# Feed-forward units of all tokens, and the features' quad at the end of the dense run, in an adaLN block with linear attention

## The chip, the cores and the metric

One core of a Trainium2 chip. The metric is the device time of one execution in microseconds; lower is better. All data are fp32, and TensorE runs each fp32 matmul as two passes (the trace shows two matmul instructions for each in the code). TensorE is PE in the profile, VectorE DVE, ScalarE ACT, GpSimd POOL, SyncE SP (it issues nearly all DMAs).

## What is computed

A transformer block on x of 2 x 2048 x 256: LayerNorm with a learned scale and shift, causal linear attention with 16 heads of 16 channels and 128 random features, a gated residual, a second LayerNorm, and a feed-forward layer with 4 low-rank experts of which each token takes 2. Cut to what matters:

```python
phi(z)  = exp(z @ omega - 0.5 * |z|^2) / sqrt(128)          # per head
S, Z    = cumsum(phi_k * v), cumsum(phi_k)                  # causal, over tokens
y       = (phi_q @ S) / (phi_q . Z + 1e-6)
x       = x + ga * (y @ W_proj + b_proj)
h       = layernorm(x) * (1 + cb) + sb
w       = softmax(h @ Wg.T + bg), kept for the top 2 of 4 experts
out_e   = relu(h @ Wi.T + (h @ A_e.T) @ B_e.T) @ Wo.T       # hidden size 1024
x       = x + gb * sum_e w_e * out_e
```

Since only two experts count for a token, the kernel computes `relu(base + low_0)` and `relu(base + low_1)`, scales the input so that the first has weight 1, multiplies the second by rho (the ratio of the two weights), and adds them before the second layer.

## The kernel before

The tokens are worked in 8 blocks of 512 (i = 0 to 7), the heads in 4 groups of 4, and each block in 8 rounds (k = 0 to 7): a round is one head group and two chunks of 128 tokens. `keep_written_order` ties every engine to the order of the code, so what is written first on an engine runs first.

A round has a part of *dense* matmuls (full 128 x 128 array; `run_full`) and a part of *tiled* ones: `scores` (L481, four column tiles; for the next round's chunks), and `outputs` (L503: the sums for the states, ps, L521; on VectorE the new states S, L529 and L531; then the products with the scores, L538, and with the states, L544). ScalarE copies the result (y, L550). Then come the *features* of a later group, a quad of four matmuls on four row tiles (L446), whose exponentials ScalarE takes (L457), and the masks of the scores on VectorE (L497).

The dense part works on three blocks at once. For a = i + 1 it makes queries and keys (`query_key`, L350: matmul, VectorE's scaling L361, ScalarE's Square L364, two DMAs to DRAM) and values (`values`, L420); for i it transposes the keys (`turn`, which is `keys` L464 and the copy `keep_keys` L475); for p = i - 1 `project`, `norm2_stats`, `channels2` (transposes, then L322 on VectorE), `router`, `choose` (some 20 small VectorE instructions that pick the experts), `low_rank` (transposes of choose's result, L693), `weigh` (L701); for q = i - 2 the second feed-forward layer `finish` (L765, one token tile: 16 passes, then L777 on VectorE).

The first feed-forward layer runs in four *units* per block: half of its 8 channel tiles for half of its 512 tokens. A unit is `hidden` (L726: four banks, 8 matmuls of 256 columns), `first` (`low_step` on four row tiles, L721; four Relus on ScalarE, L749) and `second` (`low_step` again, four products with rho on VectorE, L762, four adds on GpSimd, L763). Units 1 to 3 of block q run in rounds 0, 1, 2 and unit 0 of block p in round 7; in between stand values and `turn`.

PSUM has eight banks: two hold the scores, four have the tag "mm" (`mm_tile`), two the tag "side" (`side_tile`). A unit takes all four mm banks, and so do the features. `outputs` takes both side banks; query_key, values, project and finish take one each; `turn` takes two of either kind, as it is told.

`behind(i, 5)` issues `choose(p)` and then `norm1_stats(i + 2)` on VectorE. After the last block, units, `finish` and `finish_last` of the last two blocks follow in a tail.

```python
run_full(i, k, turn)
if k == 5 and i:
    router(i - 1, mm_tile if i in (1, N - 1) else side_tile)
...
if following:
    scores(*following)
outputs(i, g, (t, t + 1))
gi, gg = divmod(n // NT + 1 + k % 2, NG)
if gi < N:
    exponentials(*features(gi, gg, k % 2))
```

Of the kernel before, what the change touches and what calls it, by code (L numbers as in the profile page):

```python
# [32 lines left out]
def kernel(  # L33
# [469 lines left out]
    def outputs(i, g, ts):  # L503

        sums, ys = (side_tile(f"{nm}{i}_{g}{ts[0]}") for nm in ("ps", "py"))
        rows = [slice(j * HW, (j + 1) * HW) for j in range(HG)]
        cols = [slice(j * VW, (j + 1) * VW) for j in range(HG)]
        v = st[i]["v"]  # L510
        before, added = [], []
        for t in ts:
            s0 = (t % 2) * P
            ps, kt = sums[:, s0 : s0 + HG * VW], turned.pop((i, g, t), None)
            before.append(None if i % NBLK == 0 and t == 0 else S[g])
            if kt is None:
                continue
            for j in range(HG):
                for c in range(4):
                    cg = slice(c * CG, (c + 1) * CG)  # L520
                    nc.tensor.matmul(  # L521
                        ps[cg, cols[j]], kt[:, j, cg], v[:, t, g * HG + j, 0:VW],
                        start=True, stop=True,
                    )
            S[g] = work.tile([P, HG * VW], FP, tag=f"S{g}", name=f"S{i}_{g}{t}", bufs=3)
            added.append((S[g], ps, before[-1]))
        for new, ps, old in added:
            if old is None:
                nc.vector.tensor_copy(new, ps)  # L529
            else:  # L530
                nc.vector.tensor_add(new, ps, old)  # L531
        if ts[0] == 0:
            y[g] = work.tile([P, TB], FP, tag="y", name=f"y{i}_{g}")
        for t, state in zip(ts, before):
            tok = slice(t * P, (t + 1) * P)
            py, am = ys[:, (t % 2) * P : (t % 2 + 1) * P], staged.pop((i, g, t))
            for j in range(HG):
                nc.tensor.matmul(  # L538
                    py[rows[j], :], v[:, t, g * HG + j, :], am[:, j, :],
                    start=True, stop=state is None,  # L540
                )
            if state is not None:
                for j in range(HG):
                    nc.tensor.matmul(  # L544
                        py[j * HW : j * HW + VW, :], state[:, cols[j]], phi[i, g, 0, j][:, tok],
                        start=False, stop=True, tile_position=(0, j * HW),
                    )
        for t in ts:
            tok, py = slice(t * P, (t + 1) * P), ys[:, (t % 2) * P : (t % 2 + 1) * P]
            nc.scalar.copy(y[g][:, tok][:, ::-1] if t % 2 else y[g][:, tok], py)  # L550
        if ts[-1] == NT - 1:
            if g == 0:
                st[i]["ydr"] = dram.tile([NG, HG, 2, DH, TB], FP, tag="ydr", name=f"ydr{i}")
            nc.sync.dma_start(st[i]["ydr"][g].rearrange("j s d t -> (j s d) t"), y[g])
# [168 lines left out]
                start=False, stop=True, skip_group_check=True, tile_position=(HW * j, 0),  # L723
            )

    def hidden(i, u, banks=None):  # L726

        s = st[i]
        f0, t0 = RG * (u % 2), TH * (u // 2)
        ts = slice(t0, t0 + TH)  # L730
        banks = [b[:, 0:TH] for b in banks or [mm_tile(f"ph{i}_{u}{j}") for j in range(RG)]]
        for j, ph in enumerate(banks):
            f = f0 + j
            for k in range(KC):
                nc.tensor.matmul(  # L735
                    ph, wi_sb[:, k, f * P : (f + 1) * P], s["h2"][:, k, ts],
                    start=(k == 0), stop=False, skip_group_check=True,
                )
        s["unit"][u] = (banks, f0, ts)

    def first(i, u):
        s = st[i]
        banks, f0, ts = s["unit"][u]
        low_step(s, 0, banks, f0, ts)
        r = [
            work.tile([P, 2, TH], FP, tag="r", name=f"r{i}_{u}{n}") for n in range(2)
        ]
        for j, ph in enumerate(banks):
            nc.scalar.activation(r[j // 2][:, j % 2, :], ph, AF.Relu)  # L749
        s["unit"][u] = (banks, f0, ts, r)  # L750

    def second(i, u):

        s = st[i]
        banks, f0, ts, r = s["unit"].pop(u)
        low_step(s, 1, banks, f0, ts)
        for j, ph in enumerate(banks):
            f = f0 + j
            if f not in s["g"]:
                s["g"][f] = work.tile([P, TB], FP, tag="g", name=f"g{i}_{f}", bufs=NF)  # L760
            g = s["g"][f][:, ts]
            nc.vector.scalar_tensor_tensor(g, ph, 0.0, s["rho"][:, ts], ALU.max, ALU.mult)  # L762
            nc.gpsimd.tensor_add(g, g, r[j // 2][:, j % 2, :])  # L763

    def finish(i, t, tile=side_tile, f0=0, f1=NF):  # L765

# [72 lines left out]
    def run_full(i, k, turn):  # L839


        a, p, q = i + 1, i - 1, i - 2
        late = a == N
        unit = None
        if (q >= 0 and k < 3) or (p >= 0 and k == 7):
            unit = (q, k + 1) if k < 3 else (p, 0)
        n = ({1: 2, 2: 0, 3: 3, 7: 1} if i == 0 else {0: 2, 1: 0, 2: 3, 7: 1}).get(k)
        if i == 0 and k == 0:
            values(0, 2)
            values(0, 3)  # L850
        if a < N and k == (i == 0):
            channels1(a)

        turned_here = (i, k) in ((0, 1), (1, 0), (1, 4))
        if turned_here:
            turn(mm_tile if k < 2 else side_tile)
        if p >= 0 and k == 3:
            project(p, 0, NT)
            norm2_stats(p)
        if q >= 0:  # L860
            t = ({4: 2, 6: 3} if late else {4: 0, 5: 1, 6: 2, 7: 3}).get(k)
            if t is not None:
                finish(q, t)
                if t == 3:
                    store(q)
        if p >= 0:
            if k == 4:
                channels2(p)
            elif k == 6 and q >= 0:
                low_rank(p)  # L870
        t = ({4: 0, 5: 1, 6: 2, 7: 3} if i == 0 else {0: 0, 1: 1, 2: 2, 7: 3}).get(k)
        if p >= 0 and k == 7:
            if q < 0:
                query_key(a, n)
                low_rank(p)
                values(a, t)
            weigh(p)
            if q < 0:
                turn(side_tile)
                turned_here, n, t = True, None, None  # L880
        last_keys = (0, 1)
        if late and unit and k < 3:

            if k == 0:
                turn(side_tile, (0,))
                last_keys = (1,)
            else:
                finish(q, k - 1, side_tile, 0, RG)
        if unit and k == 0:
            hidden(*unit)  # L890
        if a < N and n is not None:
            query_key(a, n)
        if unit and k:
            hidden(*unit)
        if unit:
            first(*unit)
        if late and k in (1, 2):
            finish(q, k - 1, None, RG)
        if a < N and t is not None:
            values(a, t)  # L900
        if i == 0:
            if k in (4, 5):
                gate(k - 4, 0)
            elif k == 6:
                columns(1)
        elif i == 1 and k in (1, 4):
            gate(k // 4, 1)
        if not turned_here:
            on_side = unit or (k == 5 and (late or i == 1)) or (i, k) == (1, 6)
            turn(side_tile if on_side else mm_tile, last_keys)  # L910
        if unit:
            second(*unit)

    def amid(i, k):

# [41 lines left out]
    for i in range(N):  # L957
        for k in range(PAIRS):
# [7 lines left out]
                    keep_keys(i, g, t + n)  # L966

            run_full(i, k, turn)
            if k == 5 and i:
                router(i - 1, mm_tile if i in (1, N - 1) else side_tile)  # L970
            following = [chunk_at(m) for m in (n + 2, n + 3)] if n + 2 < TOTAL else []
            if following:
                scores(*following)
            outputs(i, g, (t, t + 1))

            gi, gg = divmod(n // NT + 1 + k % 2, NG)
            if gi < N:
                exponentials(*features(gi, gg, k % 2))
            for chunk in following:
                mask(*chunk)  # L980
# [13 lines left out]
        return pa + [side_tile(f"{name}{n}") for n in range(2)]  # L994

    divide_invert(p)
    hidden(q, 1, other_set("last1"))
    first(q, 1)
    hidden(q, 2)
    second(q, 1)  # L1000
    first(q, 2)
    hidden(q, 3, other_set("last3"))
    second(q, 2)
    first(q, 3)
    divide(p)
    finish(q, 0, mm_tile)
    second(q, 3)
    project(p, 0, NT)
    norm2_stats(p)
    finish(q, 1, mm_tile)  # L1010
# [7 lines left out]
    store(q)  # L1018
    low_rank(p)
    weigh(p)  # L1020
    hidden(p, 0)
    first(p, 0)
    hidden(p, 1, other_set("end1"))
    second(p, 0)
    first(p, 1)
    hidden(p, 2)
    second(p, 1)
    first(p, 2)
    hidden(p, 3, other_set("end3"))
    second(p, 2)  # L1030
    first(p, 3)
    finish_last(p, 0, 0, NF)
    second(p, 3)
    finish_last(p, 1, 0, NF)
    for f0 in (0, RG):
        for t in (2, 3):
# [48 lines left out]
```

## Time and profile before

| | us |
|---|---|
| median of 3 runs | 807.51 (801.08 to 807.72) |
| the profiled execution | 797.27 |
| its span, first to last instruction | 795.5 |
| TensorE busy, matmuls | 762.6 |
| VectorE, ScalarE, GpSimd busy | 381.8, 323.5, 137.6 |
| mean granted TensorE clock | 0.996 |

A block takes about 93 us in the middle of the kernel. The profile is of one execution. A group's "mean ns" is the duration of one instruction; matmuls are pipelined, so neighbours overlap and the distance from start to start is shorter (216 ns for a 256-column pass whose own duration is shown as about 380 ns). "[0.32 <-DVE v L431]" at the end of a line says that the engine sat idle for 0.32 us before it, and what ended that.

### The profile page before, as it was taken

To read this page: it belongs to the slowest core of one execution; us is meant where nothing else is said; L and a number is where in the kernel's file an instruction comes from. 1 tells how busy PE (TensorE), PEld (TensorE's weight loads), DVE (VectorE), ACT (ScalarE), POOL (GpSimd) and SP (SyncE) were. 2 spreads that over 40 slices of the span, in tenths; PEclk is the share of its full clock that TensorE was granted. 3 is DMA by queue.
4 is the path that set the end of the run, shared out by engine and by line. 5 is a ranking of instruction groups with operands and counts; after the bars stand their busy time and mean duration, and the time that the engine had idled before them with its cause. 6 is when DMAs were issued, how large, how long until landed. Compare 5 with 4: busy or idle time off the path is not lost.

```text
span 795.5 us, 30312 instructions
## 1 busy us (share of the span) xinstructions
PE 762.6 (96%) x13648; PEld 560.4 (70%) x13648; DVE 381.8 (48%) x1068; ACT 323.5 (41%) x700; POOL 137.6 (17%) x182
## 2 busy tenths in 40 slices
PE   9988999899999999999999999999999999999998
PEld 6555767476787667766687667777677767777766
DVE  5735558734445435543456344354364324543622
ACT  2644545434343354444444344444444343432020
POOL 3100300112101311121201121013130012004122
PEclk9999999999999999999999999999999999999999
DMA  4477243033221342023321332213230130012000
GB/s 127 123 232 247 77 153 115 23 92 108 69 82 47 104 132 84 16 82 113 105 69 36 95 105 81 69 49 115 85 106 16 55 98 16 16 42 70 2 26 28
DMA packets 44257, 65.84 MB, mean 83 GB/s; under 512 B 6752, under 2 KB 20256, under 8 KB 44128
## 3 DMA queue, kind: packets, MB, share of 16 engines
q1 hardware_dynamic: 42240, 62.33, 24.8%
q8 instruction: 107, 1.75, 0.9%
q10 hardware_dynamic: 1888, 1.58, 0.6%
q14 instruction: 22, 0.18, 0.1%
HBM read 35.32 MB, written 28.57 MB: 80 GB/s over the span
## 4 chain that ended last, share of the span: by engine, by line
PE 88%; DVE 4%; issue 3%; ACT 0%; ACTq 0%
PE pf L772 12%; PE ph L735 12%; PE pa L488 9%; PE pp L446 9%; PE pq L354 7%; PE pk L470 6%; PE ph L721 5%; PE ps L521 4%; PE py L538 4%; PE po L597 4%; PE py L544 4%; PE pv L427 4%; PE pf L794 2%; PE pw L707 1%; PE ptf L311 1%
## 5 line engine op out<-in xcount | busy, mean ns | idle before, releaser
L457 ACT ACTIVATE phi<-pp,lnm 128x512 f32<-128x512 f32 x256 | 154.9, 688 | 41.5 <-PE pp L446 41.5
L763 POOL TENSOR_TENSOR g<-g,r 128x256 f32<-128x256 f32 x128 | 90.4, 738 | 364.2 <-DVE g L762 324.5
L772 PE MATMUL pf<-wo_g,g 128*128 128x256 f32 x448 | 104.5, 385 | 0.2 <-DVE g L762 0.2
L735 PE MATMUL ph<-h,wi_sb 128*128 128x256 f32 x448 | 102.3, 381 | 1.8 <-DVE h L712 1.5
L772 PEld LDWEIGHTS pf<-wo_g,g 128*128 128x128 f32 x448 | 82.7, 190 | 29.0 <-issue 14.1
L735 PEld LDWEIGHTS ph<-h,wi_sb 128*128 128x128 f32 x448 | 84.0, 190 | 22.6 <-issue 5.1
L550 ACT COPY y<-py 128x128 f32<-128x128 f32 x128 | 27.8, 269 | 163.0 <-PE py L544 158.7
L488 PEld LDWEIGHTS pa<-phi,phi 128*32 128x32 f32 x4096 | 77.2, 110 | 14.9 <-issue 13.4
L478 ACT COPY kt<-pk 128x512 f32<-128x512 f32 x120 | 66.8, 592 | 49.6 <-PE pk L470 48.8
L488 PE MATMUL pa<-phi,phi 128*32 128x64 f32 (+3 forms) x4096 | 86.1, 235 | 0.0
L497 DVE TENSOR_TENSOR am<-pa,causal 128x512 f32<-128x512 f32 x128 | 82.3, 681 | 6.6 <-PE py L538 5.6
L446 PE MATMUL pp<-f,om 32*128 32x512 f32 x512 | 78.4, 655 | 0.6 <-issue 0.6
L470 PE MATMUL pk<-ident,phi 128*128 128x128 f32 x480 | 67.7, 276 | 1.5
L762 DVE SCALAR_TENSOR_TENSOR g<-ph,rho 128x256 f32<-128x256 f32 x112 | 39.6, 416 | 60.2 <-PE ph L721 60.2
L470 PEld LDWEIGHTS pk<-ident,phi 128*128 128x128 f32 x480 | 55.1, 141 | 16.3 <-issue 5.8
L544 PE MATMUL py<-phi,S 128*17 128x128 f32 x960 | 54.3, 275 | 10.0 <-issue 6.8
L749 ACT ACTIVATE r<-ph 128x256 f32<-128x256 f32 x112 | 34.0, 387 | 72.2 <-PE ph L721 62.9
L354 PE MATMUL pq<-hT,w_sb 128*128 128x512 f32 x120 | 59.6, 619 | 2.3 <-issue 1.8
L538 PE MATMUL py<-am,v 128*32 128x128 f32 x1024 | 56.4, 276 | 2.3 <-issue 2.2
L521 PE MATMUL ps<-v,kt 128*32 128x17 f32 x3840 | 48.7, 186 | 5.2 <-issue 4.3
L531 DVE TENSOR_TENSOR S<-ps,S 128x68 f32<-128x68 f32 x112 | 25.6, 228 | 54.2 <-PE ps L521 52.3
L431 DVE TENSOR_TENSOR v<-pv,bv_bc 128x256 f32<-128x256 f32 x32 | 13.5, 424 | 75.9 <-PE pv L427 75.6
(144 smaller groups left out, 834.2 us busy)
## 6 DMA issues: line engine op xcount, KB each, us to landing
f<-qd SPq DMA_DIRECT2D x60, 256.0 KB
qd<-qs SPq DMA_DIRECT2D x58, 256.0 KB
ydr<-y SPq DMA_DIRECT2D x32, 256.0 KB
num<-ydr SPq DMA_DIRECT2D x16, 256.0 KB
inv<-rdr SPq DMA_DIRECT2D x16, 256.0 KB
xt<-in_x_dram SPq DMA_DIRECT2D x7, 512.0 KB
out_dram<-xt SPq DMA_DIRECT2D x7, 512.0 KB
wo_g<-in_woT_dram SPq DMA_DIRECT2D x2, 1024.0 KB
```

The lines of the kernel that those rows point to most:

```text
L354: nc.tensor.matmul(pq, w_sb[:, k, n * P : (n + 1) * P], s["hT"][:, k, :], start=(k == 0), stop=(k == KC - 1),)
L446: nc.tensor.matmul(pp, om[rs, :], f[rs, :], start=True, stop=True, tile_position=(2 * DH * j, 0))
L457: nc.scalar.activation(ph, pps[j], AF.Exp, bias=lnm)
L470: nc.tensor.transpose(pk[:, j * P : (j + 1) * P], phi[i, g, 1, j][:, t * P : (t + 1) * P], ident)
L488: nc.tensor.matmul(pa[t % 2][c * CG : (c + 1) * CG, j * P + q0 : j * P + q1], phi[i, g, 1, j][:, t0 + c * CG : t0 + (c + 1) * CG], phi[i, ...
L497: nc.vector.tensor_mul(am, pa[t % 2][:].rearrange("p (h q) -> p h q", h=HG), causal[t % 2][:].unsqueeze(1).to_broadcast([P, HG, P]),)
L521: nc.tensor.matmul(ps[cg, cols[j]], kt[:, j, cg], v[:, t, g * HG + j, 0:VW], start=True, stop=True,)
L538: nc.tensor.matmul(py[rows[j], :], v[:, t, g * HG + j, :], am[:, j, :], start=True, stop=state is None,)
L544: nc.tensor.matmul(py[j * HW : j * HW + VW, :], state[:, cols[j]], phi[i, g, 0, j][:, tok], start=False, stop=True, tile_position=(0, j * HW),
L735: nc.tensor.matmul(ph, wi_sb[:, k, f * P : (f + 1) * P], s["h2"][:, k, ts], start=(k == 0), stop=False, skip_group_check=True,)
L763: nc.gpsimd.tensor_add(g, g, r[j // 2][:, j % 2, :])
L772: nc.tensor.matmul(po, s["g"][f][:, t * P : (t + 1) * P], wo_g[i // NBLK][:, f, :], start=(f == 0), stop=(f == NF - 1), skip_group_check=True,
```

## The change

Two things. First, the units: blocks whose units run inside the rounds have two *large* units (half of the channel tiles for all 512 tokens, so matmuls, Relus, products and adds of 512 columns), in round 1 of block q and in round 7 of block p; rounds 0 and 2 have none. In a large unit two of the four products are kept back and issued in `outputs`, behind the updates of S. The last block and the tail keep units of 256 tokens. Second, the features: where `ahead` holds, which is in all rounds without a unit, they are issued right after `run_full`, ahead of `router`, `scores` and `outputs`, and their exponentials stand ahead of the y copies on ScalarE. The dense part is now a table of steps, and with it the order in the dense part and the choice of banks for `turn` change: values of a block go to rounds 1 and 7 (two each), `finish` to rounds 2, 4, 6 and 7, and in rounds 2, 4, 5 and 6 the keys use side banks.

```diff
@@ outputs, behind the updates of S
+        for keep, j in kept_back:
+            keep(j)
+        kept_back.clear()
@@ units
-        f0, t0 = RG * (u % 2), TH * (u // 2)
-        ts = slice(t0, t0 + TH)
+    def small(u):
+        return RG * (u % 2), TH * (u // 2), TH
+    def large(u):
+        return RG * u, 0, TB
+        f0, t0, w = unit
+        ts = slice(t0, t0 + w)
@@ first
-            work.tile([P, 2, TH], FP, tag="r", name=f"r{i}_{u}{n}") for n in range(2)
+            work.tile([P, 2, w], FP, tag="r", name=f"r{i}_{f0}{t0}{n}") for n in range(2)
@@ second
-        for j, ph in enumerate(banks):
+        def keep(j):
...
+            nc.vector.scalar_tensor_tensor(g, banks[j], 0.0, s["rho"][:, ts], ALU.max, ALU.mult)
             nc.gpsimd.tensor_add(g, g, r[j // 2][:, j % 2, :])
+        now = RG if w < TB else RG // 2
+        for j in range(now):
+            keep(j)
+        kept_back.extend((keep, j) for j in range(now, RG))
@@ run_full
+        mm, side = (turn, mm_tile), (turn, side_tile)
         if i == 0:
+            steps = (
+                (mm, (values, 0, 2), (values, 0, 3)),
+                ((channels1, a), mm, (qk, 2)),
+                (mm, (qk, 0)),
+                (mm, (qk, 3)),
+                (mm, (gate, 0, 0), (v, 0)),
+                (mm, (gate, 1, 0), (v, 1)),
+                (mm, (columns, 1), (v, 2)),
+                (mm, (qk, 1), (v, 3)),
+            )
+        elif i == 1:
+            steps = (
+                ((channels1, a), mm, (qk, 2), (v, 0)),
+                (mm, (gate, 0, 1), (qk, 0), (v, 1)),
+                (mm, (qk, 3)),
+                (mm, (projection,)),
+                ((gate, 1, 1), side, (channels2, p)),
+                (side,),
+                (side,),
+                ((low_rank, p), (v, 2, 3), (weigh, p), side, (unit, p, large(0), (qk, 1))),
+            )
+        elif a < N:
+            steps = (
+                ((channels1, a), mm, (qk, 2)),
+                ((qk, 0), (unit, q, large(1), (v, 0, 1), side)),
+                ((qk, 3), side, (ff, 0)),
+                (mm, (projection,)),
+                ((ff, 1), (channels2, p), side),
+                (side,),
+                ((ff, 2), (low_rank, p), side),
+                ((ff, 3), (weigh, p), (qk, 1), (unit, p, large(0), (v, 2, 3), side)),
+            )
+        else:
+            steps = (
+                ((turn, side_tile, (0,)), (unit, q, (RG, 0, TH), (turn, side_tile, (1,)))),
+                ((ff, 0, side_tile, 0, RG),
+                 (unit, q, (RG, TH, TH), (ff, 0, None, RG), side)),
+                ((ff, 1), side),
+                (mm, (projection,)),
+                ((ff, 2), (channels2, p), side),
+                (side,),
+                ((ff, 3), (low_rank, p), side),
+                ((weigh, p), (unit, p, small(0), side)),
+            )
@@ the round
             run_full(i, k, turn)
+            gi, gg = divmod(n // NT + 1 + k % 2, NG)
+            ahead = not (k == 7 and i >= 1 or i >= 2 and k == 1 or i == N - 1 and k == 0)
+            if gi < N and ahead:
+                exponentials(*features(gi, gg, k % 2))
             if k == 5 and i:
-                router(i - 1, mm_tile if i in (1, N - 1) else side_tile)
+                router(i - 1)
...
             outputs(i, g, (t, t + 1))
-            gi, gg = divmod(n // NT + 1 + k % 2, NG)
-            if gi < N:
+            if gi < N and not ahead:
                 exponentials(*features(gi, gg, k % 2))
```

In a unit's step, what stands behind the unit's name runs between `first` and `second`; `ff` is `finish` of block q (and `store` after tile 3), `v` is `values` and `qk` `query_key` of block a.

## The prediction

> **What bounds the kernel now.** I read the page first (engine totals, the chain that ended last, the groups), then the waits of TensorE, then the timeline of single stretches of the fifth block (i = 4, 340 to 445 us), and last a place in the final block that already runs in the new order.
>
> ```profile
> PE 762.6 (96%) x13648; PEld 560.4 (70%) x13648; DVE 381.8 (48%) x1068; ACT 323.5 (41%) x700; POOL 137.6 (17%) x182
> ...
> PE 88%; DVE 4%; issue 3%; ACT 0%; ACTq 0%
> ```
>
> TensorE is busy 96% of the span and is 88% of the chain. In the waits of TensorE by releaser nearly all is "issue" (6.8, 4.3, 2.2 and 1.8 us), and all that names another engine is under 10 us. So the sum is simple: TensorE time taken out is gained, and every new wait of TensorE is lost in full. VectorE (48%) and ScalarE (41%) matter only where they return a PSUM bank or an operand too late. There are six banks to give: four "mm" and two "side". A tile gets a bank when its former user has been read out.
>
> **What it takes out**, per block of 8 rounds (i = 2 to 5). Start to start in the trace, a dense pass of 256 columns takes 216 ns and one of 512 takes 429 (each fp32 matmul is two passes). `hidden`: 64 x 216 becomes 32 x 429 ns, 13.82 to 13.73, 0.1 us. `low_step`: a quad of 256 columns takes 0.645 us (391.36 to 392.01); the features' quad, the same kind at 512 columns, 1.07. Eight quads become four: 5.16 to 4.28, 0.9 us. Moving the features: the last pass before a change between dense and tiled matmuls is 93 ns longer (309 for 216, 202 for 109). Dense to row tiles goes from 8 changes to 10, dense to column tiles from 4 to 0: 0.2 us. That outputs are now followed by dense work costs nothing: the last state quad takes 0.36 us before the features and also at the one place where dense work follows (698.89 to 699.26). In each round with a unit, the second key transpose waits about 0.3 us for VectorE to read the values (0.32 at 390.78) and the first starts 0.1 late; two such rounds instead of four save 0.8. Together 2.0 us per block.
>
> The Trainium skill ("TensorEngine Tiling (Array Packing)", Key Properties) says that a change of tiling mode drains TensorE, which gives the 93 ns a reason and speaks for the change; it names no price. Counted by that rule alone, the block falls from 36 changes to 30, and at the row's 93 ns the whole change would be worth 0.6 us a block.
>
> **What it adds: rounds 1 and 7 (the units).** Of the unit's four products, two are made before the S updates and two behind them; only then are the four mm banks free for the features, which stay last in these rounds. The same place in round 2 before (columns: start, duration, engine, line, operation):
>
> ```profile
> 392.01 1.33 PE L488 MATMUL pa<-phi,phi 128*32 128x128 f32 x64
> 392.10 1.42 DVE L762 SCALAR_TENSOR_TENSOR g<-ph,rho 128x256 f32<-128x256 f32 x4 [1.37 <-PE ph L721]
> ...
> 393.96 0.23 DVE L529 COPY S<-ps 128x68 f32<-128x68 f32 x1 [0.45 <-PE ps L521]
> 394.23 0.23 DVE L531 TENSOR_TENSOR S<-ps,S 128x68 f32<-128x68 f32 x1
> ...
> 394.59 1.14 PE L446 MATMUL pp<-f,om 32*128 32x512 f32 x8
> ```
>
> Count from the start of scores (392.01). The four products of 256 columns are done at +1.50, well before the features at +2.58. A product of 512 columns isn't in this trace. Its nearest row is L497, PSUM times SBUF over 128x512: 681 ns, 0.60 apart (two in 1.28); the other bound is two of L762, 0.67 apart. I take 0.60. Two run from +0.09 to +1.37 and delay nothing; S ends at +2.45 as before; the other two end at +3.05 and +3.65. The fourth matmul of the features' quad waits for the last bank until about +3.73 instead of starting at 2.58: 1.15 us (1.1 to 1.3), twice a block: 2.3. Behind that matmul stands the whole next round on TensorE; behind the two late products on VectorE stand the masks (and `divide`), which are read a round later. The Relus grow from 387 ns to about 592 (L478, a copy of 512 columns, is the nearest row; 0.57 apart): 2.4 us, under two values and two transposes of 3.0 us: nothing; without that cover it would be 0.6. GpSimd's adds (738 ns for 256 columns) may double to 1.5 us, so 5.9 us per unit; the second layer comes some 8 us later: nothing.
>
> Against this edit stands a rule: "If Scalar/Vector aren't saturated, but are causing bubbles on other engines, breaking up instructions may allow work to be completed sooner" (Trainium skill, "Perfetto Trace Analysis", Optimizing Scalar/DVE Operations). By that page's 125 ns per VectorE instruction on PSUM, merging would save 0.5 us of VectorE a unit (an estimate), and the wait would be nearer 0.9 than 1.15 us.
>
> **Round 2** is now query_key, transposes on side banks, finish of tile 0. Side banks alternate: the query takes one, the first transpose the other, the second transpose waits for the query's, `finish` for the first transpose's.
>
> ```profile
> 383.12 1.98 PE L354 MATMUL pq<-hT,w_sb 128*128 128x512 f32 x4
> ...
> 385.20 0.75 DVE L361 TENSOR_SCALAR qs<-pq,bqk 128x512 f32<-128x512 f32 x1 [2.28 <-ACT phi L457]
> ...
> 385.98 0.63 ACT L364 ACTIVATE qs<-qs 128x512 f32<-128x512 f32 x1 [0.36 <-DVE qs L361]
> ```
>
> From the query's start (0): its matmuls take 1.72 us, the first transpose 0.44, so the second could start at 2.16. VectorE has the query at 2.83, so it starts at 2.9: 0.75 lost. ScalarE's Square stands ahead of the key copy in its queue: Square to 3.49, copy (592 ns) to 4.0. `finish` could start at 3.34 and starts at 4.07: 0.73 lost. Together 1.5 us (0.75, if a bank of the other tile came first). Before, 3.55 us of `hidden` lay in between.
>
> **Round 6.** `low_rank` needs `choose`, 20 VectorE instructions at the end of round 5. Before, the features' quad (1.07) and `finish` (3.56) covered them, to the tenth of a microsecond:
>
> ```profile
> 421.96 3.72 PE L772 MATMUL pf<-wo_g,g 128*128 128x256 f32 x16
> ...
> 425.10 0.46 DVE L682 COPY los<-los 128x216 f32<-128x216 f32 x2
> ...
> 427.80 0.42 DVE L777 TENSOR_TENSOR xt<-pf,xt 128x256 f32<-128x256 f32 x1
> ```
>
> The features now come before the scores, so `finish` alone covers. The last block has no features in round 5, and shows what that costs:
>
> ```profile
> 699.26 3.72 PE L772 MATMUL pf<-wo_g,g 128*128 128x256 f32 x16
> ...
> 703.68 1.09 PE L693 MATMUL pl<-ident,los 128*128 128x128 f32 x8 [0.70 <-DVE los L682]
> ```
>
> 4.42 us from the start of `finish` to `low_rank`, not 3.56: 0.86 lost. Then the keys go to side banks, and the second transpose needs the bank of `finish`. Its reader (L777) stands behind choose and norm1_stats on VectorE and ended at 428.22, 7.33 us after the round-5 outputs ended (420.89); TensorE is there at 5.73. The loss is 1.67; it is 1.1 if that tile gets the first transpose's bank instead, whose copy waits behind two lT copies (L698); 0 if neither. I take 1.25, so 2.1 for the round. The mm banks that the keys used before were free.
>
> **Small ones.** Round 4: the features' fourth bank waits for the second h2 transpose (read out at 409.71, 5.72 us after its `finish` began; TensorE is there at 5.40): 0.4. Round 5: the second transpose waits for y copies that end 0.57 us after the outputs, 0.44 after its partner: 0.2. Rounds 0 and 3: nothing; exponentials end before the outputs, and divide's DMAs keep 5 us of slack (ydr issued 355.31, den loaded from 357.34, needed 8 us later). The two queue copies per query stay on SP in the same order.
>
> **Sum.** Blocks 2 to 5: 2.3 + 1.5 + 2.1 + 0.4 + 0.2 = 6.5 lost, 2.0 gained: +4.5 each, +18. Block 6 has no norm1_stats behind choose: 5.2 - 2.0 = +3.2. Block 7 keeps its units: +0.3. Blocks 0 and 1: gates' and h2's banks now hold up the features (VectorE reads a gate bank for about 1.4 us, values cover 0.9: 0.5 three times; h2 1.3 once), the first transposes wait for the exponentials (0.8): +3.5, between 0 and 6. In all +25. Profiled execution: 795.5 us span, 797.3 with what lies around: 822. The median shown, 807.5, is 1.3% above it: 832.
>
> **Rivals.** *The banks come in time, only the gains count* (faster). Place: features of rounds 1 and 7, and round 6. It decides where waits stay under 2.0 us per block; price 2.0 on five blocks and about 0.5 elsewhere, 797. For it: VectorE is half idle. Against: it is busy exactly there, and two waits of 1.15 alone exceed the gain. 8%. *Only the units' waits come* (same): 2.3 - 2.0 = +0.3 per block, and with +0 to 3.5 at the start about 810. It needs other bank choices in rounds 2 and 6, where the second side bank leaves none. 8%. *Instruction supply* (still slower): "issue" waits of 15.1 us fall in the tiled bursts, which now have less dense work between them (round 5 falls to about 5.5 us); half as many again gives +7.5, 840. 14%. The forecast itself: 70%, its own range 819 to 841.
>
> **Range and chances.** With the low ends (round 6's second wait 0, round 2 at 0.75, start 0) +13, so 820; with the high ends about +33, 840, and the runs spread by 0.8%. To hold 8 in 10 the range reaches down into the case of no change: 808 to 846. Within 1% (about what a measurement can tell) 8%, faster 8%, slower 84%.
>
> **What would show it.** L721 with 512 columns at 1.07 a quad; L446 in rounds 1 and 7 idle 1.1 for DVE g; L470 waiting for DVE qs in round 2 and for DVE xt or ACT kt in round 6; L693 waiting for DVE los by 0.86 in every block. Rounds 2 and 6 without idle TensorE would make this wrong.

## The result, and the profile after

| | before | after |
|---|---|---|
| median, us | 804.94 (4 runs, 801.08 to 807.72) | 827.30 (4 runs, 822.74 to 828.58) |
| ratio to before, 95% interval | | 1.0271 (1.0204 to 1.0338) |
| span of the profiled execution, us | 795.5 | 824.8 |
| mean granted TensorE clock in it | 0.996 | 0.989 |

The change makes the kernel slower by 2.7%, 22 us. Medians here are over all executions, while the ratios leave out those more than 1.5% above the fastest of the same kernel, which changes a number for one kernel only, the one with four causes undone. The first part of the page after, and the shares of the chain that ended last:

```profile
PE 773.2 (94%) x13296; PEld 531.6 (64%) x13296; DVE 380.5 (46%) x1024; ACT 320.7 (39%) x656; POOL 131.5 (16%) x138
...
PE 85%; DVE 10%; issue 4%; ACT 1%; POOL 0%; POOLq 0%; DVEq 0%
```

TensorE has 352 matmul instructions fewer and is still the bound, but VectorE's share of the chain went from 4% to 10%: TensorE now waits for it. The waits of TensorE after (releaser, us in total, times, longest):

```profile
PE py L541 <- issue: 9.7, 7, 4.0
PE ps L521 <- issue: 8.1, 6, 1.6
PE pl L696 <- DVE los L685: 5.0, 6, 0.9
PE pk L470 <- DVE qs L361: 3.4, 5, 1.0
PE pk L470 <- ACT kt L478: 3.1, 4, 0.8
PE pf L793 <- ACT kt L478: 2.9, 5, 0.6
PE py L547 <- DVE S L531: 2.7, 1, 2.7
```

Before, the longest line that names another engine was this one:

```profile
PE py L544 <- DVE S L531: 2.6, 3, 1.9
```

After, five stand above it. The last of them is a single wait ahead of block 2, and the other four are the places that the prediction named: `low_rank` behind choose, the second key transpose of round 2 behind the query's bank, the second transpose of round 6 and `finish` of round 2 behind key copies. The features' wait isn't in the list, as it falls inside a burst of matmuls; the timeline shows it. Round 7 of block 4, a round with a large unit (start, duration, engine, line):

```profile
468.87 1.33 PE L488 MATMUL pa<-phi,phi 128*32 128x128 f32 x64
468.95 1.29 DVE L777 SCALAR_TENSOR_TENSOR g<-ph,rho 128x512 f32<-128x512 f32 x2 [1.80 <-PE ph L724]
...
471.23 1.28 DVE L777 SCALAR_TENSOR_TENSOR g<-ph,rho 128x512 f32<-128x512 f32 x2
471.59 0.67 PEld L446 LDWEIGHTS pp<-f,om 32*128 32x128 f32 x6 [0.21 <-issue]
471.59 2.09 PE L446 MATMUL pp<-f,om 32*128 32x512 f32 x8
...
472.56 0.29 PEld L446 LDWEIGHTS pp<-f,om 32*128 32x128 f32 x2 [0.31 <-DVE g L777]
```

The quad's last two weight loads wait for the second pair of products, and eight passes that took 1.14 us before last 2.09. From the quad's start to the next dense matmul it is 2.02 us, not 1.07.

Round 2 of block 4:

```profile
402.69 1.98 PE L354 MATMUL pq<-hT,w_sb 128*128 128x512 f32 x4
...
404.93 0.74 DVE L361 TENSOR_SCALAR qs<-pq,bqk 128x512 f32<-128x512 f32 x1
...
405.71 0.63 ACT L364 ACTIVATE qs<-qs 128x512 f32<-128x512 f32 x1 [1.46 <-DVE qs L361]
405.73 0.66 PE L470 MATMUL pk<-ident,phi 128*128 128x128 f32 x4 [0.62 <-DVE qs L361]
...
406.95 3.69 PE L793 MATMUL pf<-wo_g,g 128*128 128x256 f32 x16 [0.57 <-ACT kt L478]
```

The second transpose starts when VectorE has read the query, and `finish` when ScalarE has copied the first transpose, with the Square ahead of the copy in its queue. The two transposes take TensorE 2.44 us here. Before, they took 1.27 in this round, which held a unit and a wait for VectorE's reading of the values, and without any wait they take 0.87 (the kernel with mm keys in round 2, below).

Round 6 of block 4:

```profile
439.09 3.72 PE L793 MATMUL pf<-wo_g,g 128*128 128x256 f32 x16
...
443.20 0.46 DVE L685 COPY los<-los 128x216 f32<-128x216 f32 x2
443.62 1.06 PE L696 MATMUL pl<-ident,los 128*128 128x128 f32 x8 [0.80 <-DVE los L685]
...
445.90 0.66 PE L470 MATMUL pk<-ident,phi 128*128 128x128 f32 x4 [0.78 <-ACT kt L478]
```

4.53 us from the start of `finish` to `low_rank`; before, it was 3.56. The second transpose waits once more, for a key copy on ScalarE.

Adding up TensorE's time from each matmul's start to the next one's start, by what the matmul does (us in the whole kernel):

| stage | before | after | |
|---|---|---|---|
| features | 75.0 | 86.5 | +11.5 |
| key transposes | 65.5 | 77.0 | +11.5 |
| second layer (holds the wait of `low_rank` behind it) | 116.1 | 121.4 | +5.3 |
| state sums and outputs | 122.4 | 128.6 | +6.2, mostly "issue" |
| the low-rank quads of the units | 45.2 | 39.4 | -5.9 |

The other stages sum to a change of less than 1 us, none of them to more than 2.0. The merging saves what it should; the first three rows cost nearly five times as much. Not all of it belongs to the middle of the kernel: from round 0 of block 2 on the rows change by +8.1, +8.8, +5.3, +0.8 and -4.4 us, so nearly all that the outputs lost, and a quarter of the first two rows, lies ahead of it.

**Where in the kernel.** Views of the windows, before and then after (stretch, its length, TensorE busy and matmuls, granted clock, DMA share, GB/s):

```profile
0.00:179.00 179.00, 164.49 (x3260) 0.98 0.43 132
...
400.00:600.00 200.00, 196.56 (x3830) 1.00 0.26 81
```

```profile
0.00:179.00 179.00, 160.79 (x3085) 0.96 0.39 121
...
400.00:600.00 200.00, 189.74 (x3365) 1.00 0.25 78
```

From block 2 on the clock is full in both to the two digits shown, so what differs there is work and waits: in the same 200 us TensorE is busy 6.8 us less. I cut each trace at the first score matmul of round 0 of block 2. The part behind the cut, called the *steady part* below, is 616.3 us before and 637.1 after. It has to be read with two corrections: after, the features of that round stand ahead of its scores, so 1.07 us of the same work has moved to the front of the cut, and the first `values` of the block, 0.86 us, have moved behind it, into round 1. The rise is 20.8 + 1.07 - 0.86 = 21.0 us. By block (start of the scores of round 0 to the next): blocks 2 to 5 rise by 2.9, 3.8, 3.8 and 3.9 us, the last two blocks and the tail together by 6.4; the outputs of those two blocks take 3.0 us of that.

### The profile page after: what moved, and what is told of

Its sections match the earlier page's. It is cut to its first block, busy times and chain, and to the rows that moved or that the text cites. A ratio compares the mean times of both kernels' runs of the same rounds, so it can differ in the third digit from the quotient of the medians.

```text
span 824.8 us, 29425 instructions
## 1 busy us (share of the span) xinstructions
PE 773.2 (94%) x13296; PEld 531.6 (64%) x13296; DVE 380.5 (46%) x1024; ACT 320.7 (39%) x656; POOL 131.5 (16%) x138
## 4 chain that ended last, share of the span: by engine, by line
PE 85%; DVE 10%; issue 4%; ACT 1%; POOL 0%; POOLq 0%; DVEq 0%
PE ph L745 12%; PE pf L793 10%; PE pa L488 10%; PE pp L446 9%; PE pk L470 6%; PE pq L354 6%; PE ps L521 4%; PE ph L724 4%; PE py L541 4%; PE pv L427 3%; PE po L600 3%; PE py L547 3%; DVE am L497 2%; PE pf L815 2%; DVE num L593 1%
## 5 line engine op out<-in xcount | busy, mean ns | idle before, releaser
L778 POOL TENSOR_TENSOR g<-g,r 128x512 f32<-128x512 f32 (+1 forms) x84 | 84.1, 1035 | 336.7 <-DVE g L777 299.0
L745 PE MATMUL ph<-h,wi_sb 128*128 128x512 f32 (+1 forms) x272 | 101.6, 527 | 1.6 <-DVE h L715 1.5
L446 PE MATMUL pp<-f,om 32*128 32x512 f32 x512 | 90.0, 642 | 0.1
L488 PE MATMUL pa<-phi,phi 128*32 128x96 f32 (+3 forms) x4096 | 87.1, 236 | 1.4 <-DVE sc L641 0.8
L478 ACT COPY kt<-pk 128x512 f32<-128x512 f32 x120 | 67.1, 590 | 54.4 <-PE pk L470 53.1
L745 PEld LDWEIGHTS ph<-h,wi_sb 128*128 128x128 f32 x272 | 52.2, 194 | 48.9 <-issue 40.5
L470 PE MATMUL pk<-ident,phi 128*128 128x128 f32 x480 | 71.6, 284 | 11.1 <-DVE qs L361 3.4
L760 ACT ACTIVATE r<-ph 128x512 f32<-128x512 f32 (+1 forms) x68 | 30.2, 526 | 99.5 <-PE ph L724 90.2
L777 DVE SCALAR_TENSOR_TENSOR g<-ph,rho 128x512 f32<-128x512 f32 (+1 forms) x68 | 36.7, 590 | 45.5 <-PE ph L724 45.5
```

The source lines that it names most:

```text
L446: nc.tensor.matmul(pp, om[rs, :], f[rs, :], start=True, stop=True, tile_position=(2 * DH * j, 0))
L470: nc.tensor.transpose(pk[:, j * P : (j + 1) * P], phi[i, g, 1, j][:, t * P : (t + 1) * P], ident)
L488: nc.tensor.matmul(pa[t % 2][c * CG : (c + 1) * CG, j * P + q0 : j * P + q1], phi[i, g, 1, j][:, t0 + c * CG : t0 + (c + 1) * CG], phi[i, ...
L745: nc.tensor.matmul(ph, wi_sb[:, k, f * P : (f + 1) * P], s["h2"][:, k, ts], start=(k == 0), stop=False, skip_group_check=True,)
```

## The experiments

Each is compared with runs of the kernel before from the same series (their medians: 808.33, 805.69 and 807.87); the change itself stands at 1.0271. In the timed runs only differences of about 1% are safe. For the short ones I also give the steady part of the profiled execution, where the mean granted clock was within 0.02 of full in all of them.

**The two halves of the change, each alone.** The large units without any move of the features. In the kernel before:

```diff
-        if (q >= 0 and k < 3) or (p >= 0 and k == 7):
-            unit = (q, k + 1) if k < 3 else (p, 0)
+        if late:
+            which = {0: small(1), 1: small(3), 7: small(0)}.get(k)
+        else:
+            which = {1: large(1), 7: large(0)}.get(k)
```

Two products are kept back behind S; the features stay last in every round, and the keys of round 0 are turned ahead of the query.

> The kernel before with large units in rounds 1 and 7 (two products kept back), features last in every round, finish and values where they were; only in round 0 the keys go ahead of the query. If the features' place and the new order cost most: units gain 0.9 (low-rank quads) and 0.3 to 0.6 (waits of the keys), lose 1.9 (features' banks) and up to 0.8 (Relus less covered) per block, 805 to 812. Rival, that the large units are the cause: 820 or more.

Measured: 807.36 us, 1.0018 (0.9980 to 1.0056), as expected. The stages show why it is neither faster nor slower: the low-rank quads fall from 45.2 to 43.1 us and the keys from 65.5 to 62.7, and the features rise from 75.0 to 83.4. The units about pay for their own wait (the steady part is 618.1 us, 1.8 above before), no more; part of what the keys gain comes from turning them first in round 0, not from the units. The saving of the quads is smaller than in the change, since without two values between the Relus and the second quad, that quad waits up to 0.7 us, and in block 1, paced by the Relus, it then takes 2.5 us instead of 1.07.

The other half, the features moved in rounds 3 to 6 of blocks 2 and later, with small units and the old dense order:

```diff
+            ahead = i >= 2 and k in (3, 4, 5, 6)
+            if gi < N and ahead:
+                exponentials(*features(gi, gg, k % 2))
...
-            if gi < N:
+            if gi < N and not ahead:
```

> The kernel before, small units, with the features moved ahead of scores and outputs in rounds 3 to 6 of blocks 2 to 7 and nothing else. Theory: the features wait for the key copies, since both need the four mm banks: 0.9 us in each of these rounds, and low_rank waits for choose by 0.9 once: 4.6 us per block, +24, 829. Rival, that the features' place is free and the cost lies in the new banks and order: 808 +- 3.

Measured: 826.47 us, 1.0269 (1.0236 to 1.0301): as much as the whole change. Its steady part is 637.3 us, 21.0 above before. A group kept apart by shape (count, busy time, mean ns, idle before; the busy time was 78.4 us before), a moved quad in round 3 of block 4, and a line of its waits:

```profile
L446 PE MATMUL pp<-f,om 32*128 32x512 f32 x512 | 94.9, 654 | 2.3 <-issue 2.3
```

```profile
412.55 1.97 PE L446 MATMUL pp<-f,om 32*128 32x512 f32 x8
...
413.40 0.29 PEld L446 LDWEIGHTS pp<-f,om 32*128 32x128 f32 x2 [0.20 <-ACT kt L478]
```

```profile
PE pl L693 <- DVE los L682: 4.2, 5, 0.9
```

The quads in the moved rounds take 1.90 to 1.96 us instead of 1.07, since they now need mm banks that the key transposes held a moment ago and ScalarE has to copy first: features +18.2 us in the stages. `low_rank` waits for choose in four more blocks, and the second layer's row, which holds that wait, rises by 4.2. 18.2 + 4.2 = 22.4 us is the loss, within 1.5. The change itself puts the keys of rounds 4 to 6 on side banks and so keeps the quads of rounds 5 and 6 at 1.07 and that of round 4 at 1.43, but then the keys of rounds 5 and 6 wait there, 1.2 us per block, and those of round 2 more. So in rounds 3 to 6 the move costs with either kind of bank, though by other waits, and that both kernels end at the same time is partly chance. A reason that fits both, though only argued, is that a dense part that ends with the features asks for six banks in a row where the old order left a stretch of scores and outputs for reading them out.

**Round 2: only the kind of bank.** In the kernel after:

```diff
-                ((qk, 3), side, (ff, 0)),
+                ((qk, 3), mm, (ff, 0)),
```

> In round 2 the keys' transposes go to mm banks, nothing else changes (the instructions and their order are the same). If the bank rotation is the cause: the second transpose no longer waits for VectorE's query (0.85) nor finish for the key copy (0.6), 1.5 us in each of blocks 2 to 6, -7.5 us (820). Rival, that TensorE's loss only moves on: the features that end the round wait for the key copies instead, since they need the same four mm banks, and the time stays within 2 us of 827.

Measured: 820.10 us, 1.0165 (1.0111 to 1.0220); steady part 627.4 us, 9.7 below the change, 8.1 of it in the key transposes (77.0 to 68.1 us in the whole kernel). The same place in its timeline:

```profile
404.63 1.04 PE L470 MATMUL pk<-ident,phi 128*128 128x128 f32 x8
...
405.50 3.62 PE L793 MATMUL pf<-wo_g,g 128*128 128x256 f32 x16
```

`finish` starts 0.87 us behind the first transpose. The order of the instructions is the same on every engine, so the waits of round 2 are the banks' and nothing else's, and they are worth about a third of the whole loss (7.2 of 22.4 us by the medians, though the two intervals just overlap).

**Round 6: cover for `low_rank` again.** In blocks 2 and later the features of round 6 go back to the end, and the keys, on mm banks, stand between `finish` and `low_rank`:

```diff
-                ((ff, 2), (low_rank, p), side),
+                ((ff, 2), mm, (low_rank, p)),
...
-            ahead = not (k == 7 and i >= 1 or i >= 2 and k == 1 or i == N - 1 and k == 0)
+            ahead = not (k == 7 and i >= 1 or i >= 2 and k in (1, 6) or i == N - 1 and k == 0)
```

> In round 6 of blocks 2 to 6 the keys are transposed (on mm banks) between finish and low_rank, and the features stay last in this round. If choose's length is the cause: the transposes (0.97 us) cover what the features covered before, L696 waits under 0.1 instead of 0.9, and the second transpose no longer waits 1.0: -1.9 us per block, -9 us (818). Rival, that the wait passes to the second queue step: the scores' sums wait for key copies behind the lT copies, and under 4 us come back.

Measured: 823.95 us, 1.0196 (1.0136 to 1.0256); steady part 633.5 us, 3.6 below the change. The waits on L696 fall from 5.0 to 0.7 us and those of the keys on L478 vanish, so both waits are what they were taken for. Of some 9 us only about 3.5 came out in the steady part. From one round's scores to the next, the stretch to round 6 fell by 2.7 to 2.9 us in blocks 2 to 4 (from 11.86 to 8.92 in block 3), of which 1.07 is the features, which moved to the next stretch, but by 1.3 and 0.3 in blocks 5 and 6. In those two `finish` of round 6 took 5.24 and 4.93 us instead of 3.56, and the granted clock was 0.87 there (528 to 541 us and 628 to 641 us): 3.1 us that this one execution lost to the clock and not to a wait. So in the trace the two waits are worth nearer 7 us than 3.5; the timed runs show 3.4 us by the medians and 6 by the ratios. The next stretch rose by 1.07 in three blocks and by 2.5 and 1.9 in two; that surplus is idle time of TensorE in the outputs that the profile puts down to "issue". Why it comes there wasn't found.

**Rounds 1 and 7: the products kept back.** All four products at once, ahead of S:

```diff
-        now = RG if w < TB else RG // 2
+        now = RG
```

> All four products of a large unit before the updates of S, none kept back. If the wait of the features in rounds 1 and 7 is set by VectorE's last product: the banks are free about 2.5 us after the start of scores, the features' quad falls from 2.02 to 1.07 us, but S ends about 0.6 us later and the second chunk's state products wait for it by about 0.5: 0.45 less per unit, 11 units, -5 us against the changed kernel (822). Rival, that keeping two back is what holds the loss down: the outputs wait by 1 us or more for S, 0 to +6 us.

Measured: 826.82 us, 1.0266 (1.0201 to 1.0332): no difference. Two of its waits of TensorE:

```profile
PE ps L521 <- issue: 12.8, 7, 2.8
...
PE py L547 <- DVE S L531: 5.1, 11, 2.7
```

The features' quad is short again (group L446: 80.5 us in all, 90.0 in the change), but the outputs wait for S 11 times instead of once, and "issue" ahead of the state sums took 4.7 us more. The wait moves from the features to the outputs.

The banks can also be freed without the products: ScalarE takes the Relu of the two banks into `g`, and VectorE multiplies by rho later, from SBUF.

```diff
-            nc.vector.scalar_tensor_tensor(g, banks[j], 0.0, s["rho"][:, ts], ALU.max, ALU.mult)
+            if j < now:
+                nc.vector.scalar_tensor_tensor(g, banks[j], 0.0, s["rho"][:, ts], ALU.max, ALU.mult)
+            else:
+                nc.vector.tensor_mul(g, g, s["rho"][:, ts])
...
+        for j in range(now, RG):
...
+            nc.scalar.activation(s["g"][f0 + j][:, ts], banks[j], AF.Relu)
```

> The two kept-back products of a large unit are split: ScalarE's Relu reads the bank into g at once (about 0.6 us each, beside VectorE's two products), and VectorE multiplies g by rho behind S from SBUF. If the bank's return is the whole of the loss in rounds 1 and 7: quad 2.02 to 1.07 us, 0.95 less per unit, 11 units, -10 us (817). Rival, that ScalarE is late itself (key copies stand ahead of the Relus, sums wait for them): under 4 us.

Measured: 842.57 us, 1.0441 (1.0392 to 1.0490), 15 us slower than the change though the features' quads of rounds 1 and 7 are back at 1.07. VectorE's product from two SBUF operands, as a group:

```profile
L780 DVE TENSOR_TENSOR g<-g,rho 128x512 f32<-128x512 f32 x22 | 25.1, 1181 | 0.0
```

and two waits of TensorE behind it:

```profile
PE pk L470 <- DVE qs L361: 12.4, 5, 2.7
...
PE pq L354 <- DVE hT L322: 5.4, 6, 1.1
```

The product that it replaces takes 684 ns in the change. Of four of these in one block, the one begun between two of GpSimd's adds took 680 ns, and the three begun during an add 919, 1636 and 1750. VectorE falls behind and is late for the query (L361) and for h (L322). To see whether that is the cause, the same with the product on GpSimd:

```diff
-                nc.vector.tensor_mul(g, g, s["rho"][:, ts])
+                nc.gpsimd.tensor_mul(g, g, s["rho"][:, ts])
```

> As the kernel with two Relus on ScalarE, but the product of these two with rho is made by GpSimd (two more GpSimd instructions per unit, about 1.3 us each), so VectorE has no SBUF-times-SBUF product beside GpSimd's adds. If the 842.6 us came from VectorE's products, which took 1.18 us in the mean there and 0.68 at best, beside GpSimd: quad 1.07, query and finish in round 2 no later than in the changed kernel, 818 (-9). Rival, that the slowing is GpSimd's own length (7.7 us of work per unit) and finish waits for g: 827 or more.

Measured: 824.64 us, 1.0250 (1.0206 to 1.0293); steady part 632.9. The 18 us between the two go with VectorE's slow products, the only difference: TensorE's wait for the query falls from 12.4 to 5.3 us, and that for h from 5.4 to 0.5. The change has 3.4 in the first of these, and the rest of the gain isn't there. A likely reason is `divide`'s product, which stands ahead of the query on VectorE in round 2, also has two operands in SBUF and slows down further beside GpSimd's longer work (1354 ns against 1100, last section).

**The start.** Blocks 0 and 1 of the change in the old order, features last there:

```diff
-            ahead = not (k == 7 and i >= 1 or i >= 2 and k == 1 or i == N - 1 and k == 0)
+            ahead = i >= 2 and not (k in (1, 7) or i == N - 1 and k == 0)
```

The step tables of these blocks go back too, for instance:

```diff
-                (mm, (qk, 0)),
-                (mm, (qk, 3)),
+                ((qk, 0), mm),
+                ((qk, 3), mm),
```

> The changed kernel, with the order and the features of the kernel before in blocks 0 and 1 (round 7 of block 1 keeps its large unit). If the 8.4 us that the first two blocks lost in the profile come from the features standing between VectorE's results and the next transposes, and behind the gates' banks: -5 to -8 us (820 to 822). Rival, that they come from instruction supply, which the order doesn't set: within 2 us of 827.

Measured: 825.54 us, 1.0265 (1.0230 to 1.0300): within the spread. In the profiled executions the cut at block 2 came at 182.2 us instead of 187.7. How far one such number can be trusted is told by the kernel with the features alone: up to the cut it runs the same instructions as before, and reached it at 185.5 us, not 179.3. With the two corrections of the cut made where they apply, the six executions with the old start (before, this one, each half alone and the two kernels below) lie between 179.3 and 193.6 us, 185.0 in the mean, and the six with the new one (the change and the five variants above) between 187.2 and 191.5, 188.6 in the mean. So the new start costs 3 to 4 us by the means, which is less than the executions with one and the same start differ among themselves; the timed runs confirm only that it isn't large.

**Four causes undone at once.** The change with mm keys in round 2, round 6 as above, the Relus on ScalarE with the product on GpSimd, and the old start. The features stay ahead in rounds 0 and 2 to 5 of blocks 2 and later. Beside those edits the rule for them becomes:

```diff
-            ahead = not (k == 7 and i >= 1 or i >= 2 and k == 1 or i == N - 1 and k == 0)
+            ahead = i >= 2 and not (k in (1, 6, 7) or i == N - 1 and k == 0)
```

> The changed kernel with four causes taken away at once: keys of round 2 on mm banks, round 6 with the keys between finish and low_rank and the features last, the two kept-back products split between ScalarE's Relu and GpSimd, and blocks 0 and 1 as before. Features stay ahead in rounds 0, 2, 3, 4 and 5 of blocks 2 to 7. If the waits add up and nothing else costs: the four alone gave -7.2, -3.4, -2.7 and -1.8 in the medians, together at least -15, 812; by the waits they remove in the traces (7.5, 9, 9 and 5) up to -28, 799, which is below the kernel before. Rival, that TensorE is bound by something else once the waits are gone (instruction supply, which showed 20 to 26 us of idle in these kernels and 16 before): 815 or more.

Measured: 810.27 us (12 runs), 0.9988 (0.9948 to 1.0028; from seven of the runs, whose median is 808.84). In the timed runs the loss is gone and no gain is left. That the four causes are the whole of it isn't shown. This kernel also has the units' banks freed by ScalarE, and the next version, which has that too but leaves the features last, ran 7.9 us faster in the same series. And the one trace, of a long execution (814.3 us), doesn't have the time back: the waits for VectorE and ScalarE at the four places are gone, but its steady part is 626.8 us, 10.5 above before, with 21.0 us of "issue" waits of TensorE where before had 7.5. Whether these belong to the kernel or to that execution is open, and so is why each cause alone gave back less than its waits.

**A version faster than both.** Large units without the move of the features, and the two banks freed by ScalarE with the product on GpSimd, so that the units' own wait goes as well; the first values of blocks 2 to 6 are moved from round 0 to round 1. On top of the edit for the units alone:

```diff
+                nc.gpsimd.tensor_mul(g, g, s["rho"][:, ts])
...
+            nc.scalar.activation(s["g"][f0 + j][:, ts], banks[j], AF.Relu)
...
+        if i >= 2 and k == 0:
+            t = None
+        elif i >= 2 and k == 1 and a < N:
+            values(a, 0)
```

> Large units alone, features last in every round (807.4 in the earlier run), with the two kept-back products split between ScalarE and GpSimd and the first values of blocks 2 to 6 moved from round 0 into the unit's gap in round 1. If the features' bank wait (0.95 per unit) and the uncovered Relus (0.3) are what the large units cost: -9 to -12 us, 796 to 799, faster than the kernel before by about 1%. Rival, that GpSimd's longer work beside VectorE's products takes it back: 804 or more.

Measured: 802.38 us (12 runs), 0.9928 (0.9897 to 0.9960), against 807.87 before in the same series. The features are back at 75.4 us in the stages, the low-rank quads at 42.0, and the steady part is 612.7. The gain of 0.7% is clear of the interval, but it is half of what was expected (796 to 799 us); the time lies between that and the rival. It is the half of the change that can be made useful, with a bank return and an order of the values that the change doesn't have.

## Why the prediction was right

The forecast was 832 (819 to 841 for the case itself) and the median is 827.3; on the profiled execution 822 was forecast and 826.5 came. The mechanism is the one that the prediction describes: where it said that TensorE would wait, TensorE waits, for the reader that was named. Its terms, per block, with what the trace after shows in block 4:

| term | forecast, us | measured, us |
|---|---|---|
| features' quads in rounds 1 and 7 | 2 x 1.15 | 2 x 0.95 |
| round 2, both waits | 1.5 | 1.57 |
| round 6, `low_rank` behind choose | 0.86 | 0.97 |
| round 6, second transpose | 1.25 (0, 1.1 or 1.67) | 1.0 |
| round 4 | 0.4 | 0.37 |
| round 5 | 0.2 | 0.23 |
| together | 6.5 | 6.0 |
| net of the gains, blocks 2 to 5 | +4.5 each | +2.9, +3.8, +3.8, +3.9 |

**Units.** The product of 512 columns, taken at 0.60 us apart by the row of the masks, comes two in 1.28 or 1.29: that term was right. The quad costs 0.2 less than forecast: 0.95. Its last weight load comes 3.69 us after the start of the scores, where 3.73 was said, but the quad itself starts at 2.72 us and not at 2.58; so the bank's time was right, and "1.15 us (1.1 to 1.3)" was too narrow. The Relus, the adds on GpSimd and the second layer cost nothing visible, as said; the kernel with the units alone shows what the cover of the two values was worth.

**Round 6.** The bank was the other one of the two cases left open: the second transpose waits for the first transpose's copy on ScalarE, not for L798 (L777 before). Its price was the 1.1 that stood for this case, 1.0 measured. The forecast took a middle value where the order of the side tiles in the round decides between the cases.

**Gains.** 6.0 less a mean rise of 3.6 leaves gains of 2.4 us per block, against 2.0. The low-rank quads gave 0.87 in each of blocks 2 to 5, where 0.9 was said; the rest of their 5.9 us lies elsewhere, 1.5 of it ahead of block 2. What goes beyond 2.0 is in the outputs, which took 0.3 to 1.2 us less per block, by shorter "issue" waits, and the forecast had no term for that.

**Sizes off.** Blocks 2 to 5 gave 14.4 of the forecast 18, and the last two blocks and the tail 6.4 instead of 3.5; there "issue" waits in the outputs of block 6 went from 0.2 to 4.4 us. The start was put at 3.5 with bounds of 0 and 6; 8.4 us stand in the two traces, 0.2 of which is the cut, and executions with one and the same code there differ by 6. One wait of the start was sized wrongly: the features of round 4 of block 1, which the banks of a gate and of h2 hold up, were to lose 0.5 and 1.3 us there, and took 4.35 instead of 1.07, part of it while the granted clock was low (0.76 over 136 to 150 us). That the sum came so near owes something to luck, since these errors have opposite signs: less in blocks 2 to 5, more at both ends. The step from the profiled execution to the median added 1.3% to the whole, and for the change there was no such step (826.5 and 827.3); without it the forecast would have stood at 822, below the median and no longer above it. The profiled execution of before lay below all its timed runs (797.3 against 801 to 808), that of the change among its own (826.5 in 822.7 to 828.6). The 29.3 us between the two spans therefore overstate the change, and the 22.4 between the medians is the better figure.

**Rivals.** *Only the units' waits come* (forecast 810) is what the kernel with the units alone does: 807. That moving the features can cost as much as the rest is shown by the kernel that moves them alone, though with other banks and so by other waits. *Instruction supply* (forecast +7.5 on top) came in part: "issue" waits of TensorE in the steady part went from 7.5 to 10.7 us, those on other engines from 5.8 to 18.6. Some of it came where that rival said, at round 5: in blocks 2, 4 and 6 the outputs behind that round's scores rose from 1.66 us to 3.07 to 3.46, while outputs elsewhere in blocks 2 to 5 fell by more. *The banks come in time* fell with the first of these waits.

## What to carry to other kernels

Where one engine is busy 96% of the time, ask of each instruction that is moved what it covered: here a quad of 1.07 us between two stages helped to hide the chain that picks the experts and gave the readers of four banks their time, and both bills came due when it moved. Follow each shared bank from reader to next writer, with all that is queued ahead of that reader on its engine; in blocks 2 to 5 every wait found in that way was within 0.25 us of the trace. A merge of instructions is worth its saving only if the buffers of the larger one still come free in time, which the 807 us of the units alone and the 802 us with two banks freed by another engine show.

## What the runs showed of the hardware

**VectorE beside GpSimd.** A product on VectorE with both operands in SBUF takes longer when it begins while a GpSimd add runs; one that reads PSUM doesn't. From the groups kept apart by shape, before:

```profile
L590 DVE TENSOR_TENSOR num<-num,inv 128x512 f32<-128x512 f32 x16 | 11.7, 772 | 0.0
```

after:

```profile
L497 DVE TENSOR_TENSOR am<-pa,causal 128x512 f32<-128x512 f32 x128 | 82.3, 682 | 11.0 <-PE py L541 10.0 <-PE pa L488 0.8
...
L593 DVE TENSOR_TENSOR num<-num,inv 128x512 f32<-128x512 f32 x16 | 17.1, 1100 | 0.4 <-DMA inv<-rdr 0.4
```

and with the product on GpSimd:

```profile
L593 DVE TENSOR_TENSOR num<-num,inv 128x512 f32<-128x512 f32 x16 | 21.0, 1354 | 0.0
```

`divide`'s product (num times inv) took 772 ns before, 1100 with GpSimd's adds of 512 columns near it, 1354 with its products as well, while the masks from PSUM stayed at 681 to 682. One by one, after: the nine of the 16 that begin during a GpSimd instruction take 879 to 1756 ns, the other seven 677 to 693. The Trainium skill ("GPSIMD Engine Reference", Key points) says that GpSimd shares its SBUF interfaces with VectorE and that instructions with two SBUF inputs contend; these rows agree, and give the price.

**The clock at the start.** The granted clock was below full mostly in the first 180 us: 0.91 to 0.98 in the first 100 us of five executions, with the DMA at 0.49 to 0.52 of its time, and in the mean within 0.02 of full from block 2 on. Single drops come later too, as in round 6 of blocks 5 and 6 above (0.87 over 13 us each). Over the 42 timed executions of the kernel before (clock 0.982 to 0.996, span 799.6 to 812.1 us) 0.01 less clock goes with some 5.8 us more. So a good part of the spread of this kernel's times belongs to its first blocks, most likely, and not to what is changed further on; that wasn't tried by itself.

**Idle TensorE with nothing to wait for.** "Issue" waits in the dense bursts of small matmuls sum to 16 to 30 us per execution and differ by several us between kernels whose instructions are nearly the same. They took back parts of the gains above. Their cause stays open.
